# Spectral weights folded by column, projections in two pieces, and a new order at the start of an attention kernel

## The chip, the cores and the metric

The kernel runs on one NeuronCore of a Trainium2 chip. The metric is device time in microseconds (us) for one execution. The engines are TensorE (PE in the profile; PEld are its weight loads), VectorE (DVE), ScalarE (ACT), GpSimd (POOL) and SyncE (SP), which here only issues DMAs. Each engine takes its instructions in the order of the program and waits on semaphores for the others.

## The reference

A layer of two branches on the same normalized input, x of shape 2 x 2048 x 256:

```python
xn = layernorm(x)                                  # per row, eps 1e-5
q, k, v = xn @ wq, xn @ wk, xn @ wv                # 16 query heads, 4 key/value heads of 16
q, k = rope(q), rope(k)
attn = causal_softmax(q k^T / 4) v @ wo
w = w_freq_real + 1j * w_freq_imag                 # 256 x 256
ffn = real(ifft(fft(xn) @ w)) + bias
out = x + attn + ffn
```

The spectral branch is linear in xn, so it is one real 256 x 256 matrix, which the kernel builds from w and from tables of cosines (`dc`) and sines (`ds`) of the transform.

## The kernel before, in words

The rows are cut into 8 blocks of 512 (4 positions of each of 2 sequences, the sequences alternating). Block n goes through these steps. `load_x` brings x by SP's queue. `row_stats` (VectorE, lines 237 and 238) gives mean and variance, `row_power` (GpSimd, 243 and 244) the reciprocal deviation, `row_shift` (VectorE, 249) minus mean times that, and the norm (399) scales and shifts each row: on VectorE for block 0, on GpSimd for the others. `transpose_x` (411) and ScalarE's copy (414) give xnT; `features` projects it to keys and values together and to two halves of the queries, through the helper `product` (155), four matmuls of 32 columns; ScalarE copies the result to `raw` (427). `rotate` and `split` apply the rotary embedding and cut float32 into three bf16 parts (518 to 556), on VectorE for block 0, on GpSimd for the others; SP's queue stacks the parts into `qst` and `kst` (393).

Then each block has 4 units of 4 heads. For each unit `maxima` computes the scores once for the row maxima (PE 155, 627 and 631, VectorE 636), `spread` sends the maxima as three more rows of `qst` (671, 677, and 678, a DMA of ScalarE's queue), `scores` computes them again and ScalarE takes the exponential (PE 155, 734 and 738, ACT 745), and `values` multiplies by v (780). `put`, `gather`, `widen` and `scale` divide by the sums on GpSimd and its DMA queue. `output` adds the spectral product `po` with mff, the product with wo, and the residual (155 and 906).

The spectral matrix `mff` is built once, in `spectral_matrix`: four `left` groups (two sums, each for two column halves; result `ps_ff`) and two `right` groups (`ps_mff`), of 16 matmuls of 128 x 256 each. The result is needed by the first `output`. Its tables are loaded by GpSimd's queue in `load_late` (225), after block 0's power.

The rotary table is expanded by `expand` (eight broadcasts on VectorE, 293) from `trig`, loaded by SP, and turned by `turn` (PE 305, ACT 306). 48 transposes of the identity (968) run on TensorE at the start.

The order on every engine is the order in which a planner inside the kernel emits the pieces. It keeps a clock for each engine (`clock`), the time from which each result is there (`there`), adds an assumed cost for each piece (`use`, `send`), and at each step takes the piece that can start soonest, with rules for ties. Each piece carries a step from which it may run and one by which it should (`since`, `by`). So a changed cost or piece can move any later piece. Before the loop, a short part is written out by hand:

```python
    ones(0)
    for i in range(NI):
        row_stats(0, i)
    row_power(0)
    load_late()
    row_shift(0)
    order_weights()
```

TensorE's results go through three PSUM banks of the ring "st", and pairs of row maxima through two double banks of the ring "s".

## Time and profile before

| | |
|---|---|
| median of 3 runs | 925.84 us (924.08 to 927.47) |
| profiled execution, its own time | 926.44 us |
| its span in the profile | 924.7 us |
| PE busy | 904.6 us (98%) |
| DVE busy | 748.0 us (81%) |
| ACT busy | 653.7 us (71%) |
| POOL busy | 370.1 us (40%) |

The busy times are of one execution. A share over the whole span is a mean over stages with different limits; TensorE's matmuls overlap in the pipeline, so a busy TensorE need not be at its peak. The idle time of an engine counts only where others wait for it.

### The profile page before, as it was taken

How to read it: one execution, taken by the hardware profiler on the slowest of the kernel's cores; microseconds unless marked ns; L12 is line 12 of the kernel's file. 1: busy time of each engine (PE TensorE's matmuls, PEld its weight loads, DVE VectorE, ACT ScalarE, POOL GpSimd, SP SyncE). 2: the span in 40 equal slices, each digit the busy share in tenths (PEclk: the TensorE clock that was granted, in tenths of full speed). 3: DMA queues.
4: the chain of work that ended last, by engine and by line, in shares of the span. 5: the costliest groups of instructions: out<-in, count | busy, mean ns of one | idle time of the engine just before them, and what ended most of it. 6: DMA issues, size and time to landing. Idle time of an engine off the chain costs nothing.

```text
span 924.7 us, 38985 instructions
## 1 busy us (share of the span) xinstructions
PE 904.6 (98%) x17324; PEld 500.5 (54%) x17324; DVE 748.0 (81%) x1056; ACT 653.7 (71%) x1375; POOL 370.1 (40%) x556
## 2 busy tenths in 40 slices
PE   7999899999999999999999999999999999999997
PEld 4666565655555555555555555555455554645443
DVE  6878697789789996998995999979789988788601
ACT  3266565587757784888865777857688878588784
POOL 7298666824672424822236520311572021102111
PEclk9999999999999999999999999999999999999999
DMA  5435823341244011440002500010133001100000
GB/s 165 119 90 143 199 92 106 97 132 38 65 121 124 27 38 34 112 129 26 14 27 85 150 28 13 27 60 14 31 109 88 15 3 38 49 14 15 27 1 24
DMA packets 41992, 62.13 MB, mean 67 GB/s; under 512 B 8840, under 2 KB 32120, under 8 KB 41824
## 3 DMA queue, kind: packets, MB, share of 16 engines
q1 hardware_dynamic: 32400, 41.18, 16.5%
q0 software_dynamic: 8128, 17.69, 5.9%
q8 instruction: 135, 2.21, 1.0%
q10 hardware_dynamic: 1296, 0.79, 0.3%
q14 instruction: 33, 0.27, 0.1%
HBM read 32.75 MB, written 18.40 MB: 55 GB/s over the span
## 4 chain that ended last, share of the span: by engine, by line
PE 89%; DVE 5%; ACT 3%; issue 1%; DMA 1%; POOL 1%; ACTq 0%; SPq 0%; DVEq 0%; POOLq 0%
PE av L780 24%; PE st L155 22%; PE sm L155 17%; PE sm L631 7%; PE po L155 6%; PE ps_q L155 4%; DVE mx L636 2%; PE sp L155 2%; PE sm L627 2%; PE st L738 2%; ACT es L745 1%; PE ps_x L411 1%; PE st L734 1%; ACT es L747 1%; PE ps_m L671 0%
## 5 line engine op out<-in xcount | busy, mean ns | idle before, releaser
L636 DVE TENSOR_REDUCE mx<-sm 128x2 f32<-128x1024 f32 (+3 forms) x640 | 648.9, 1057 | 87.4 <-PE sm L631 44.1
L745 ACT ACTIVATE es<-st 128x512 f32<-128x512 f32 (+3 forms) x1194 | 552.4, 543 | 179.2 <-PE st L155 145.6
L155 PE MATMUL st<-qst,kst 115*32 115x512 bf16 (+3 forms) x4264 | 327.2, 354 | 1.1 <-ACT es L745 0.4
L780 PE MATMUL av<-es,va 128*32 128x512 f32 (+3 forms) x2560 | 299.9, 529 | 0.6 <-issue 0.3
L155 PE MATMUL sm<-kst,qst 112*32 112x512 bf16 x3072 | 239.1, 379 | 0.1
L155 PEld LDWEIGHTS <-kst 115*32 115x32 bf16 x4608 | 161.1, 95 | 140.6 <-issue 64.8
L752 POOL TENSOR_SCALAR_AFFINE_SELECT es<-es 128x256 f32<-128x256 f32 x192 | 76.7, 406 | 276.0 <-ACT es L745 234.8
L155 PEld LDWEIGHTS <-qst 112*32 112x32 bf16 x3072 | 96.0, 96 | 93.0 <-issue 64.8
L631 PE MATMUL sm<-kst,qst 112*32 112x32 bf16 (+15 forms) x2048 | 122.3, 281 | 0.3 <-issue 0.3
L627 PE MATMUL sm<-mask,ident_h 128*32 128x128 bf16 (+3 forms) x2048 | 100.2, 201 | 1.8 <-DVE mx L636 1.0
L780 PEld LDWEIGHTS av<-es,va 128*32 128x32 f32 x2560 | 85.1, 109 | 28.6 <-ACT avs L791 2.6
L631 PEld LDWEIGHTS <-qst 112*32 112x32 bf16 x2048 | 66.3, 97 | 34.3 <-issue 20.6
L627 PEld LDWEIGHTS <-ident_h 128*32 128x32 bf16 x2048 | 66.1, 96 | 32.2 <-issue 25.5
L906 DVE TENSOR_TENSOR xr<-po,xr 128x256 f32<-128x256 f32 x36 | 15.2, 424 | 51.5 <-PE po L155 49.5
L803 POOL DMA_DIRECT2D res<-avs x30 | 18.2, 606 | 82.7 <-ACT avs L791 79.9
L155 PE MATMUL ps_q<-xnT,wp 128*32 128x512 f32 x384 | 45.4, 600 | 0.0
L747 ACT ACTIVATE es<-sp 128x1024 f32<-128x1024 f32 (+3 forms) x43 | 36.6, 907 | 7.6 <-PE sp L155 7.4
L427 ACT COPY raw<-ps_q 128x512 f32<-128x512 f32 x24 | 14.1, 585 | 35.0 <-PE ps_q L155 35.0
L518 POOL TENSOR_TENSOR ra<-raw,cs 128x512 f32<-128x512 f32 (+1 forms) x21 | 27.4, 1304 | 24.2 <-ACT raw L427 23.0
L738 PE MATMUL st<-qst,kst 115*32 115x480 bf16 (+15 forms) x512 | 36.8, 284 | 0.1
L155 PE MATMUL po<-wo_sb,attT 128*32 128x256 f32 x512 | 34.4, 379 | 0.7 <-ACT attT L869 0.7
L155 PE MATMUL po<-mff,xnT 128*32 128x256 f32 x512 | 34.4, 380 | 0.0
(108 smaller groups left out, 657.0 us busy)
## 6 DMA issues: line engine op xcount, KB each, us to landing
qst<-run SPq DMA_DIRECT2D x62, 128.0 KB
res<-avs POOLq DMA_DIRECT2D x30, 256.0 KB, 3.0
run<-part SPq DMA_DIRECT2D x31, 192.0 KB
qst<-run SPq DMA_DIRECT2D x31, 192.0 KB
xt<-in_L_attn_x_dram SPq DMA_DIRECT2D x8, 512.0 KB
xr<-in_L_attn_x_dram SPq DMA_DIRECT2D x16, 256.0 KB
out_dram<-xr SPq DMA_DIRECT2D x16, 256.0 KB
sw<-raw SPq DMA_DIRECT2D x60, 64.0 KB
```

Of the source, the lines that this page charges most:

```text
L155: nc.tensor.matmul(to[q : q + QD], lhsT[:, q : q + QD], rhs, start=start, stop=stop)
L518: e.tensor_tensor(ra[c][:r], raw[c][:r], cs[j][:r, 0, :], ALU.mult)
L627: nc.tensor.matmul(to[:, at:wd], ident_h[:, q : q + QD], mask[:, q:], start=True, stop=True, skip_group_check=True,)
L631: nc.tensor.matmul(to[:, : at + QD], rows[:, q : q + QD], keys[:, : at + QD], start=False, stop=True, skip_group_check=True,)
L636: nc.vector.tensor_reduce(t["mx"][:, i, 2 * pr : 2 * pr + 2, k], ps[0][:, :, :wd], AX.X, ALU.max)
L738: nc.tensor.matmul(to[:, at:], keys[:, q : q + QD], rows[:, at:], start=False, stop=True, skip_group_check=True,)
L745: nc.scalar.activation(es[u, t, pr][:, e, lo:], ps[:, lo:], AF.Exp, scale=SCALE)
L747: nc.scalar.activation(es[u, t, pr][:, :, lo:], wide[pr][:, :, lo:], AF.Exp, scale=SCALE)
L752: nc.gpsimd.affine_select(out=es[u, t, pr][:, :, lo : lo + P], in_=es[u, t, pr][:, :, lo : lo + P], pattern=[[0, 2], [1, P]], compare_op=A ...
L780: nc.tensor.matmul(av[u][QD * h : QD * (h + 1), lo:], va[at_block[b, t // NI]][:, t % NI, h, :], es[u, t, h // 2][:, h % 2, lo:], start=(t ...
L803: nc.gpsimd.dma_start(out=res[n, c][f], in_=avs[u])
L906: nc.vector.tensor_tensor(xr[n, r][:, e, :], po, xr[n, r][:, e, :], ALU.add)
```

## The change

The load of block 0's x becomes four DMAs of 128 rows each, and each `row_stats` of block 0 waits for its own. The rotary table of positions 0 is expanded on VectorE right behind block 0's statistics, ahead of `row_shift`. `row_shift` becomes a plain product of mean and reciprocal deviation, which the norm subtracts, and it runs on GpSimd for blocks 1 to 7. `features` is emitted as two pieces, one for each half of the contraction, which the planner may separate. The spectral matrix uses the symmetry of cosine and sine in the column: GpSimd adds and subtracts the real and imaginary weights of column c and 256 - c (two copies and four sums, `fold`), so that two `left` groups (each of two pieces of 8 matmuls) and two `right` groups of 8 matmuls remain. A further table `half_sb`, of cosine's row 128 and sine's rows 1 to 127, is loaded by two more DMAs of GpSimd's queue, into a slot of the ring "es". The negated sine table is not made any more. The planner's costs follow.

```diff
@@ -164,10 +164,13 @@
     xt = {}
     def load_x(n):
-        send("sp", 512, [slot("xt")], [("xt", "in", n)])
+        at = slot("xt")
         take_slot("xt")
         xt[n] = work.tile([P, NI, D], F32, tag="xt", bufs=2, name=f"xt{n}")
-        nc.sync.dma_start(out=xt[n], in_=block_rows(n))
+        step = NI if n else 1
+        for i in range(0, NI, step):
+            send("sp", 128 * step, [at], [("xt", "in", n, k) for k in range(i, i + step)])
+            nc.sync.dma_start(out=xt[n][:, i : i + step, :], in_=block_rows(n)[:, i : i + step, :])
     take_slot("qst"), take_slot("qst")
     load_x(0)
@@ -224,6 +227,12 @@
             spec[name] = work.tile([P, NK, D], F32, tag=tag, bufs=bufs, name=name)
             nc.gpsimd.dma_start(out=spec[name], in_=src.rearrange("(c p) n -> p c n", p=P))
             send("pool", 256, (), ["spec"])
+        take_slot("es")
+        half_sb = spec["half"] = work.tile([P, D], F32, tag="es", bufs=ES, name="half_sb")
+        nc.gpsimd.dma_start(out=half_sb[0:1], in_=dft[0, P : P + 1, :])
+        nc.gpsimd.dma_start(out=half_sb[1:P], in_=dft[1, 1:P, :])
+        send("pool", 128, (), ["spec"])
+        send("pool", 128, (), ["spec"])
         nc.gpsimd.dma_start(out=wo_sb, in_=wo.rearrange("(c p) n -> p c n", p=P))
         nc.gpsimd.dma_start(out=bias_sb, in_=bias.partition_broadcast(P))
@@ -236,7 +245,7 @@
         st = work.tile([P, 6], F32, tag="bn", bufs=3, name=f"bn{n}_{i}")
         nc.vector.bn_stats(st, xt[n][:, i, :])
         nc.vector.bn_aggr(mv[n][:, i, :], st)
-        use("dve", 0.53, [("xt", "in", n)], [("mv", n)])
+        use("dve", 0.53, [("xt", "in", n, i)], [("mv", n)])
     def row_power(n):
         rstd[n] = work.tile([P, NI], F32, tag="rs", bufs=2, name=f"rs{n}")
@@ -246,10 +255,9 @@
     def row_shift(n):
         shift[n] = work.tile([P, NI], F32, tag="sh", bufs=2, name=f"sh{n}")
-        nc.vector.scalar_tensor_tensor(
-            shift[n], mv[n][:, :, 0], -1.0, rstd[n], ALU.mult, ALU.mult
-        )
-        use("dve", 0.2, [("rs", n)], [("sh", n)])
+        e, eng, us = (nc.vector, "dve", 0.2) if n == 0 else (nc.gpsimd, "pool", 0.25)
+        e.tensor_tensor(shift[n], mv[n][:, :, 0], rstd[n], ALU.mult)
+        use(eng, us, [("rs", n)], [("sh", n)])
@@ -310,58 +318,81 @@
         return expand, turn
     mff = const.tile([P, NK, D], F32, name="mff")
     def spectral_matrix():
-        wre, wim, dc, ds_ = (spec[k] for k in ("wre", "wim", "dc", "ds"))
-        neg_s = work.tile([P, NK, D], F32, tag="xr", bufs=3, name="neg_s")
-        at_ = work.tile([P, NK, D], F32, tag="xr", bufs=3, name="at_")
-        et_ = work.tile([P, NK, D], F32, tag="xr", bufs=3, name="et_")
-        nc.scalar.mul(neg_s, ds_, -1.0)
-        use("act", 0.48, ["spec"], ["neg_s"])
+        wre, wim, dc, ds_, half_sb = (spec[k] for k in ("wre", "wim", "dc", "ds", "half"))
         first_xr = used["xr"]
         for _ in range(3):
             take_slot("xr")
-        pieces = []
-        def left(o, name, dst, parts):
-            cols = slice(o * P, (o + 1) * P)
-            ps = bank(f"ps_ff{o}")[:, :D]
-            for a, (w, f) in enumerate(parts):
-                for c in range(NK):
-                    product(
-                        ps, w[:, c, cols], f[:, c, :],
-                        start=(a == 0 and c == 0), stop=(a == 1 and c == NK - 1),
-                    )
-            nc.scalar.mul(dst[:, o, :], ps, 1.0 / D)
-            through_bank(1.87, ["neg_s"], "act", 0.29, [("left", o, name)])
+        of_c, of_s, left_sb = (
+            work.tile([P, NK, D], F32, tag="xr", bufs=3, name=name) for name in ("vc", "vs", "left")
+        )
+        up, down, far = slice(1, P), slice(D - 1, P, -1), slice(P + 1, D)
+        pool = nc.gpsimd
+        folds = []
+        def fold(to, cols, one, two, op, last=False):
+            def go():
+                pool.tensor_tensor(to[:, :, cols], one, two, op)
+                use("pool", 0.75, ["spec"], ["folded"] * last)
+            folds.append(go)
+        def ends_of(to, w):
+            pool.tensor_copy(to[:, :, 0:D:P], w[:, :, 0:D:P])
+            use("pool", 0.2, ["spec"])
+        folds += [lambda: ends_of(of_c, wre), lambda: ends_of(of_s, wim)]
+        fold(of_c, up, wre[:, :, up], wre[:, :, down], ALU.add)
+        fold(of_s, up, wim[:, :, up], wim[:, :, down], ALU.add)
+        fold(of_c, far, wim[:, :, down], wim[:, :, up], ALU.subtract)
+        fold(of_s, far, wre[:, :, up], wre[:, :, down], ALU.subtract, True)
+        def left(o, a):
+            v, f = ((of_c, dc), (of_s, ds_))[a]
+            if a == 0:
+                held[o] = bank(f"ps_ff{o}")[:, :D], take_slot("st")
+            ps, k = held[o]
+            for c in range(NK):
+                product(
+                    ps, v[:, c, o * P : (o + 1) * P], f[:, c, :],
+                    start=(a == 0 and c == 0), stop=(a == 1 and c == NK - 1),
+                )
+            use("pe", 0.94, ["folded", ("st", k - ring["st"])], [("ps", k)])
+            if a == 1:
+                nc.scalar.mul(left_sb[:, o, :], ps, 1.0 / D)
+                use("act", 0.29, [("ps", k)], [("st", k), ("left", o)])
+        held = {}
+        lefts = [("left", o) for o in range(NK)]
         def right(r):
-            cols = slice(r * P, (r + 1) * P)
             ps = bank(f"ps_mff{r}")[:, :D]
-            for a, (w, f) in enumerate(((at_, dc), (et_, neg_s))):
-                for c in range(NK):
-                    product(
-                        ps, w[:, c, cols], f[:, c, :],
-                        start=(a == 0 and c == 0), stop=(a == 1 and c == NK - 1),
-                    )
+            for c, f in enumerate((dc[:, 0, :], half_sb)):
+                product(
+                    ps, left_sb[:, c, r * P : (r + 1) * P], f,
+                    start=(c == 0), stop=(c == NK - 1),
+                )
             nc.scalar.copy(mff[:, r, :], ps)
-            lefts = [("left", o, name) for o in range(NK) for name in ("at", "et")]
-            through_bank(1.87, lefts, "act", 0.29, [("mff", r)])
+            through_bank(0.94, lefts, "act", 0.29, [("mff", r)])
             if r == NK - 1:
                 for tag, k in (
-                    ("inv", 0), ("inv", 1), ("attT", 0), ("avs", 0),
+                    ("inv", 0), ("inv", 1), ("attT", 0), ("avs", 0), ("es", 0),
                     ("xr", first_xr), ("xr", first_xr + 1), ("xr", first_xr + 2),
                 ):
                     there[tag, k] = clock["pe"]
+        pieces = []
         for o in range(NK):
-            pieces.append((["neg_s"], lambda o=o: left(o, "at", at_, ((wre, dc), (wim, ds_)))))
-            pieces.append((["neg_s"], lambda o=o: left(o, "et", et_, ((wim, dc), (wre, neg_s)))))
-        lefts = [("left", o, name) for o in range(NK) for name in ("at", "et")]
-        for r in range(NK):
-            pieces.append((lefts, lambda r=r: right(r)))
-        return pieces
+            pieces.append((["folded"], ["st"], lambda o=o: left(o, 0)))
+            pieces.append((["folded"], [], lambda o=o: left(o, 1)))
+        pieces += [(lefts, ["st"], lambda r=r: right(r)) for r in range(NK)]
+        return folds, pieces
@@ -382,7 +413,7 @@
         b, j = blocks[n]
         e, eng = (nc.vector, "dve") if n == 0 else (nc.gpsimd, "pool")
         MULT, SUB, CAST, NORM = (0.72, 0.72, 0.46, 0.33) if n == 0 else (1.23, 1.13, 0.63, 0.53)
-        raw, sw, swp, part, ra, at = {}, {}, {}, {}, {}, {}
+        raw, sw, swp, part, ra, at, held = {}, {}, {}, {}, {}, {}, {}
         sends = []
         streams.append(sends)
@@ -398,7 +429,7 @@
         def norm(i):
             e.tensor_scalar(
                 xt[n][:, i, :], xt[n][:, i, :], rstd[n][:, i : i + 1], shift[n][:, i : i + 1],
-                ALU.mult, ALU.add,
+                ALU.mult, ALU.subtract,
             )
             use(eng, NORM, [("sh", n)], [("xn", n, i)])
@@ -416,18 +447,20 @@
             if c == NK - 1:
                 there["xt", n] = clock["pe"]
-        def features(c):
-            ps = bank(f"ps_q{n}_{c}")
-            for k in range(NK):
-                product(
-                    ps, wp[:, k, c, :], xnT[n][:, k, :], start=(k == 0), stop=(k == NK - 1)
-                )
+        def features(c, k):
+            if k == 0:
+                held[c] = bank(f"ps_q{n}_{c}"), take_slot("st")
+            ps, at_st = held[c]
+            product(ps, wp[:, k, c, :], xnT[n][:, k, :], start=(k == 0), stop=(k == NK - 1))
+            use("pe", 0.9, ["wp", ("xnT", n, k), ("st", at_st - ring["st"])], [("ps", at_st)])
+            if k < NK - 1:
+                return
             raw[c] = work.tile([P, SB], F32, tag="raw", bufs=3, name=f"raw{n}_{c}")
             at[c] = take_slot("raw")
             nc.scalar.copy(raw[c], ps)
-            through_bank(
-                1.83, ["wp", *(("xnT", n, k) for k in range(NK))], "act", 0.48, [("raw", "in", n, c)],
-                [("raw", at[c] - ring["raw"])],
+            use(
+                "act", 0.48, [("ps", at_st), ("raw", at[c] - ring["raw"])],
+                [("st", at_st), ("raw", "in", n, c)],
             )
             if n >= 2:
                 other_half(c)
@@ -568,7 +601,8 @@
         ]
         for c in (NK, 0, 1):
             table = [("cs", j, 1)] * (n >= 2)
-            pe.append(("pe", ["wp", *table, *xs], ["st", "raw"] + ["sw"] * (n >= 2), lambda c=c: features(c)))
+            pe.append(("pe", ["wp", *table, xs[0]], ["st", "raw"] + ["sw"] * (n >= 2), lambda c=c: features(c, 0)))
+            pe.append(("pe", [xs[1]], [], lambda c=c: features(c, 1)))
             if n < 2:
                 pe.append(("pe", [("raw", "in", n, c)], ["st", "sw"], lambda c=c: other_half(c)))
             if c == NK:
@@ -973,6 +1007,8 @@
         row_stats(0, i)
     row_power(0)
     load_late()
+    table_0 = rotary_table(0)
+    table_0[0]()
     row_shift(0)
     order_weights()
@@ -980,9 +1016,9 @@
         norms, pe, rot = project(n)
         eng = norms[0][0]
-        stats = [("dve", [("xt", "in", n)], [], lambda i=i: row_stats(n, i)) for i in range(NI)]
+        stats = [("dve", [("xt", "in", n, i)], [], lambda i=i: row_stats(n, i)) for i in range(NI)]
         stats.append(("pool", [("mv", n)], [], lambda: row_power(n)))
-        stats.append(("dve", [("rs", n)], [], lambda: row_shift(n)))
+        stats.append(("pool", [("rs", n)], [], lambda: row_shift(n)))
         s = starts
         if n > 1:
             stream([("sp", [], ["xt"], lambda: load_x(n))], s["load"], s["load"])
@@ -1002,10 +1038,10 @@
                 out_rot.append((at, at + late + 2 + k // 2, *p))
     def table(j, since):
-        expand, turn = rotary_table(j)
+        expand, turn = rotary_table(j) if j else table_0
         last = [("cs used", at_block[B - 1, j - 2])] if j >= 2 else []
         stream(
-            [("dve", last, ["raw", "raw2"], expand)]
+            [("dve", last, ["raw", "raw2"], expand)] * (j > 0)
             + [("pe", [("trx", j)], ["st"], lambda a=a: turn(a)) for a in range(2)],
             since, since + 3,
         )
@@ -1016,11 +1052,9 @@
     chain(1, early, 1)
     load_x_2 = stream([("sp", [], ["xt"], lambda: load_x(2))])
-    def spectral():
-        for needs, piece in spectral_matrix():
-            spectral_pieces.append((-1, 8, "pe", needs, ["st"], piece))
-    spectral_pieces = stream([("act", ["spec"], [], spectral)], -1, 8)
+    folds, products = spectral_matrix()
+    stream([("pool", ["spec"], [], fold) for fold in folds], -1, 4)
+    stream([("pe", *piece) for piece in products], -1, 8)
     for n in range(2, NB):
         at = next(k for k, d in enumerate(due) if d >= a_from[NG * n])
         starts = dict(load=at - 30, stats=at - 24, pe=at - 20, rot=at - 17)
```

## The prediction

> **What bounds the kernel now.** I read the page's busy shares first, then the busy time by stage, then the chain of waits in the stage that the diff touches, and last the timeline of that stage.
>
> ```profile
> PE 904.6 (98%) x17324; PEld 500.5 (54%) x17324; DVE 748.0 (81%) x1056; ACT 653.7 (71%) x1375; POOL 370.1 (40%) x556
> ...
> PE   7999899999999999999999999999999999999997
> ```
>
> TensorE is busy in all but 20.1 us of 924.7, so only three things can move the time: less TensorE work, fewer holes in it, or work at a better clock. Where the 20.1 us lie is seen by stage (busy us of PE, PEld, DVE, ACT, POOL; then the granted clock, the DMA share, GB/s):
>
> ```profile
> 0.00:14.00 14.00, 10.68 (x68) 9.39 (x72) 9.86 (x35) 4.96 (x11) 7.96 (x21) 0.92 0.62 184
> 14.00:23.70 9.70, 8.28 (x68) 2.03 (x67) 6.45 (x13) 2.58 (x5) 8.45 (x16) 0.94 0.42 134
> 23.70:46.00 22.30, 21.74 (x472) 14.05 (x464) 18.38 (x42) 6.26 (x13) 6.87 (x11) 1.00 0.43 120
> ...
> 100.00:140.00 40.00, 36.18 (x1028) 25.97 (x1029) 32.80 (x62) 24.00 (x65) 25.47 (x39) 0.96 0.47 131
> ...
> 900.00:924.70 24.70, 18.52 (x268) 8.91 (x260) 3.23 (x8) 13.08 (x17) 3.23 (x8) 0.97 0.07 23
> ```
>
> Holes: 3.3, 1.4 and 0.6 us up to 46 us, 3.8 us between 100 and 140, 6.2 us in the tail, little elsewhere. In the first row 7.1 us of the busy time is the 48 warm-up transposes, which end at 8.55. So up to 46 us about 5.3 us stand open and the rest is real work. The chain of waits there:
>
> ```profile
> 0.80 4.43 DMA xt<-in_L_attn_x_dram
> ...
> 7.90 1.06 POOL rs L244
> 8.96 0.02 issue
> 8.98 0.16 DVE sh L249
> 9.14 1.17 DVE trx L293 x6
> 10.31 0.04 issue
> 10.36 1.11 PE ps_tr L305 x8
> 11.47 0.10 issue
> 11.56 2.32 PE ps_x L411 x8
> 13.88 2.54 PE ps_q L155 x16
> ```
>
> The reader is to see that VectorE waits for GpSimd's power (1.5 us), and only then builds the rotary table (1.63 us for eight), which does not need the power at all. The norms start at 10.61, behind the table. The second thing is the clock (same columns as above):
>
> ```profile
> 8.40:10.40 2.00, 0.20 (x3) 0.04 (x1) 1.42 (x8) 1.13 (x4) 2.00 (x3) 1.00 0.00 0
> ...
> 11.40:15.00 3.60, 3.49 (x17) 1.83 (x20) 3.10 (x12) 1.90 (x4) 3.54 (x7) 0.55 0.86 281
> ```
>
> After the empty 1.81 us from 8.55 to 10.36 the clock is 0.55 for 3.6 us. The third is block 1, seen on GpSimd's and VectorE's timeline:
>
> ```profile
> 33.42 0.23 POOL L243 TENSOR_SCALAR rs<-mv 128x4 f32<-128x4 f32 x1 [10.62 <-DVE mv L238]
> ...
> 33.81 0.15 DVE L249 SCALAR_TENSOR_TENSOR sh<-mv,rs 128x4 f32<-128x4 f32 x1
> ...
> 34.78 4.30 POOL L399 TENSOR_SCALAR xt<-xt,rs,sh 128x256 f32<-128x256 f32 x8
> ```
>
> Block 1's power was done at 20.1, but its shift sits in VectorE's queue behind block 0's rotation (17.06 to 31.04) and runs at 33.81. GpSimd is empty for 10.6 us, then has block 1's norms, and from 44.5 on its rotation.
>
> **The change, part by part.** The profiled execution took 926.44 us (span 924.7 and 1.7 around it). The median of the three runs is 925.84, 0.6 less and within their spread; I sum against the execution and take the difference off the median.
>
> *Half the products.* Before, 4 left groups and 2 right groups of 16 matmuls of 128x256 each, 96 in all; after, 4 pieces and 2 groups of 8, 48 in all. Rate from the timeline, where a full group starts 0.86 us before the next one:
>
> ```profile
> 23.70 1.05 PE L155 MATMUL ps_ff<-dc,wre 128*32 128x256 f32 x16
> ...
> 24.56 1.05 PE L155 MATMUL ps_ff<-ds,wim 128*32 128x256 f32 x16
> ```
>
> 0.86 / 16 = 54 ns; 48 x 54 ns = 2.6 us less for TensorE. ScalarE loses the negation (0.63) and two evictions (0.38 each), worth nothing on a 71% engine.
>
> *What the fold adds.* On GpSimd two small copies and four sums of 2x127 columns. No such row exists (reversed source). Nearest are a 128x512 sum at 1.28 and a 256-wide scale at 0.55. Bounds 0.55 and 1.3 each; I take 0.7, so 4 x 0.7 + 0.4 = 3.2 us (2.6 to 5.6). Below nothing is excluded, since it is only added. Two more loads by GpSimd's queue, 0.72 each like their neighbours, stand ahead of wo, the bias and block 1's memsets: 1.4 us. Cover: GpSimd's 10.6 empty us. Without it block 1's norms come 4.6 us later, and TensorE with them.
>
> *First load in four.* VectorE's memsets end at 4.63, the statistics now start at 5.25 on the whole load and step at 0.53. With pieces the first can start at 4.65, and the fourth ends at 6.8 instead of 7.48 if the last piece lands by 6.2: 0.7 less. SP issues three more DMAs of 0.44, so the rotary table's load and block 1's x leave 1.3 us later. They are first needed at 6.8 and 10.5. The DMA engines are full from 3 to 7 us (share 1.07 to 1.11) and empty from 8, so all first loads still land by about 8 in whatever order. Here the Trainium skill speaks against the change: "DMA: Bandwidth & Descriptors", section Bandwidth, wants transfers batched to 1 MiB, and its section on the anatomy of one DMA gives 2.0 us fixed for each. Taken one after another, four would need 0.8 + 4 x (2.0 + 0.3) and land at 10, costing the front some 3.5 us, and the sum below would be -0.9. The row shows several loads of different queues in flight at full share, so the fixed parts should overlap. I take the row; 0 to 0.7 us gained.
>
> *Table ahead of the shift.* VectorE: statistics to 6.8, table 1.63 to 8.45, while GpSimd takes its 1.4 us to 8.3; shift 0.16, norms 1.89 to 10.5, where they now end at 12.5. That is 2.0 us. What is late next is the fourth norm, then two evictions of ScalarE (0.59 each). If the table's load came after 8.3, shift and norms would queue behind it, us for us.
>
> *The clock.* The table's transposes follow the warm-up at 8.6 with no gap to speak of. The skill's "TensorE: Matmul & The Clock Gate", section on HAM oscillation, warns only of idle gaps above about 3.4 us; by it a gap of 1.81 is harmless and closing it gains nothing. The trace differs: 0.55 right after 1.81. From the fourth norm to the first projection's end take 3.9 us now (12.5 to 16.42); at full clock two evictions, 0.3 for the transposes, 0.86 for the second half and 0.3 of latency need 2.9. So 1.0 by the row, nothing by the rule. Together the front chain is 3.0 us earlier (2.0 by the rule).
>
> *Shift on GpSimd for blocks 1 to 7.* Seven times 0.25 on an engine at 40%, 0.15 less on VectorE. Its effect is the order: power, shift and norms of block 1 follow each other, after two blocks' memsets (2.5 each) and the two loads: norms end near 22 instead of 37. The new multiply has no negation; the norm subtracts instead, same cost. The later blocks save little, except one 1.0 us wait of the shift at 228, where VectorE is on the chain.
>
> *Projections in two pieces.* The same matmuls. A PSUM bank of the three can be held between the pieces while others are scheduled, and the later pieces may be planned up to two steps later. Bounds: -1 (better mixing) to +2; no row shows it, I take 0, since two banks already let a 0.54 us eviction alternate with 0.2 us of scores.
>
> *New holes in the front.* Block 0's rotation on VectorE still takes 14 us from the first raw copy, so row maxima start near 28.5 instead of 31.46. Until then TensorE has block 0's projections, then block 1's transposes at 22, then spectral pieces when the fold ends, about 26. Between 20.8 and 23.5 there is less to do than now, when the spectral lefts (23.3 to 31.4) fill: I charge 1.2 us (0 to 4).
>
> Sum: -3.0 - 2.6 + 1.2 = -4.4 us; 922.0 for the execution, 921.4 for the median.
>
> **The rivals.** *More than that:* block 1's GpSimd work begins up to 18 us earlier, which loosens what follows. The one big later hole is
>
> ```profile
> 106.87 0.24 PE L734 MATMUL st<-mask_t,ident_h 128*32 128x128 bf16 x4 [2.19 <-issue]
> ```
>
> where a unit's maxima had been sent only at 103.19 and the clock falls to 0.66 (106 to 111). If the new order avoids it, 2.2 and some 1.4 of slow clock go: -8.0, 917.8. Against it: any new order can have such a hole of its own.
>
> *Filler only:* TensorE waits for block 0's rotation anyway, so the products saved become holes: the sum is -3.0 + 1.2 = -1.8, 924.0. For it: VectorE is busy without a break from 17 to 31. Against: block 1 now supplies some 9 us of work there.
>
> *The fold starves TensorE:* TensorE's order is fixed, and the spectral pieces stand in it where the kernel's planner expects the fold (0.75 per sum; loads of wo and bias not counted). If the fold ends 6 us after TensorE reaches them (sums at 1.3 us, another block's memsets ahead), everything behind waits: 6.0 and 1.7 of halved clock against the 4.4 gained, -4.4 + 7.7 = +3.3, 929.1. It decides from about 4 us of lag. For it: GpSimd carries 4.6 us more just there. Against: 10.6 us empty.
>
> **How the numbers follow.** The measurement tells 0.3% (2.8 us) from no change. Chances: the sum 0.50, more than it 0.20, filler 0.15, starvation 0.15. The sum's own unknowns (fold, pieces, holes, load) make it 918.5 to 925, a sixth of it inside 0.3%. Faster 0.42 + 0.20 + 0.02, same 0.08 + 0.12, slower 0.01 + 0.15. The range reaches from beyond the second case (916.5) over the third to half way into the fourth (927.5).
>
> **What would show it.** Right: the table's transposes at 8.6 and a clock near 1.0 from 11 to 15; first projection done near 13.4; block 1's norms on GpSimd before 24 and a fold of some 3.2 us behind them; 48 spectral matmuls; TensorE busy about 902, span about 920. Wrong: a spectral matmul waiting on GpSimd for more than 3 us, statistics waiting past 7 for the last piece, a halved clock after 20 us, new waits for PSUM banks, or holes of over 2 us after 46 us.

## The result, and the profile after

The changed kernel is slower: 937.79 us (932.05 to 940.0, 6 runs) against 926.83 us (924.08 to 927.66, 6 runs), a ratio of 1.0113 with an interval of 1.0082 to 1.0143. The prediction had 921.4.

The page of the changed kernel, busy time and share of each engine:

```profile
PE 903.8 (97%) x17228; PEld 495.0 (53%) x17228; DVE 748.2 (80%) x1049; ACT 653.9 (70%) x1372; POOL 397.0 (42%) x571
```

TensorE is busy 0.8 us less than before, but over a span of 935.0 us: its holes have grown from 20.1 to 31.2 us. GpSimd is busy 26.9 us more, where the prediction added some 6. By stage (busy us of PE, PEld, DVE, ACT, POOL; then granted clock, DMA share, GB/s):

```profile
0.00:14.00 14.00, 11.84 (x80) 9.65 (x80) 10.04 (x37) 5.82 (x12) 8.59 (x22) 1.00 0.61 184
14.00:23.70 9.70, 7.16 (x60) 1.73 (x60) 8.60 (x14) 1.70 (x4) 9.28 (x17) 1.00 0.57 172
23.70:46.00 22.30, 16.94 (x303) 8.80 (x307) 14.97 (x33) 4.21 (x9) 19.31 (x24) 0.85 0.31 86
...
100.00:140.00 40.00, 33.78 (x995) 22.69 (x987) 32.42 (x60) 25.04 (x67) 28.24 (x40) 0.96 0.53 136
140.00:200.00 60.00, 58.15 (x1102) 32.90 (x1093) 43.65 (x64) 30.85 (x65) 40.57 (x49) 0.97 0.34 96
```

The first row is better than before, as forecast: 1.2 us fewer holes and a whole clock. The second has 1.1 us more holes. The third has 5.4 us of holes instead of 0.6, and the clock is 0.85. Then come 2.4 us more holes from 100 to 140, and 1.9 from 140 to 200, where there were none. The chain of waits of the first 50 us (start, us, what) shows who holds TensorE up:

```profile
9.98 0.94 PE ps_x L442 x4
10.94 0.59 ACT xnT L445
11.57 1.97 PE ps_q L155 x16
13.56 0.59 ACT raw L460
...
24.26 0.57 POOL sh L259
24.83 0.14 POOL vc L347
24.98 5.32 POOL xt L430 x4
30.34 1.33 PE ps_x L442 x5
31.66 2.69 PE ps_q L155 x16
```

Four norms on GpSimd take 5.32 us on the chain. And TensorE's own rows there (start, us, operation, idle before it and for what):

```profile
26.26 0.33 PE L442 MATMUL ps_x<-ident,xt 128*128 128x128 f32 x1 [3.49 <-POOL xt L430]
27.70 0.47 PE L442 MATMUL ps_x<-ident,xt 128*128 128x128 f32 x1 [1.11 <-POOL xt L430]
29.13 0.48 PE L442 MATMUL ps_x<-ident,xt 128*128 128x128 f32 x1 [0.95 <-POOL xt L430]
30.34 1.33 PE L442 MATMUL ps_x<-ident,xt 128*128 128x128 f32 x5 [0.73 <-POOL xt L430]
```

TensorE stands 6.3 us before block 1's transposes, and block 0's row maxima stand behind them in its queue. The clock pays again right after:

```profile
26.00:30.00 4.00, 1.28 (x3) 0.50 (x3) 3.79 (x10) 0.00 (x0) 4.00 (x4) 0.56 0.39 99
30.00:34.00 4.00, 3.67 (x21) 1.59 (x25) 0.52 (x3) 1.17 (x2) 3.06 (x6) 0.58 0.77 208
```

The reason shows in the row of the norm itself, by its tile (min, median and max ns):

```profile
L430 POOL TENSOR_SCALAR xt<-xt,rs,sh x28: 1212/1215/1449, 25.0 to 660.1; 128x256 f32<-128x256 f32 x28
```

The same row before is this, for the same shape and count:

```profile
L399 POOL TENSOR_SCALAR xt<-xt,rs,sh x28: 545/548/561, 34.8 to 650.7; 128x256 f32<-128x256 f32 x28
```

A norm that multiplies and subtracts takes GpSimd 1.215 us, one that multiplies and adds 0.548 (medians). 28 x 0.667 = 18.7 us, most of what GpSimd has gained. TensorE's waits on it are 10.5 us in all, close to the growth of its holes.

### The profile page after: what moved, and what is told of

It reads as the page before. It is cut to its first block, busy times and chain, and to the rows that moved or that the text cites. A ratio compares the mean times of both kernels' runs of the same rounds, so it can differ in the third digit from the quotient of the medians.

```text
span 935.0 us, 38841 instructions
## 1 busy us (share of the span) xinstructions
PE 903.8 (97%) x17228; PEld 495.0 (53%) x17228; DVE 748.2 (80%) x1049; ACT 653.9 (70%) x1372; POOL 397.0 (42%) x571
## 4 chain that ended last, share of the span: by engine, by line
PE 85%; POOL 5%; ACT 3%; DVE 3%; DMA 2%; issue 2%; SPq 0%; ACTq 0%; POOLq 0%; DVEq 0%
PE av L814 23%; PE st L155 22%; PE sm L155 17%; PE sm L665 6%; PE po L155 5%; PE ps_q L155 4%; POOL xt L430 3%; ACT es L779 2%; PE sp L155 2%; PE sm L661 1%; DVE mx L670 1%; PE st L772 1%; PE ps_x L442 1%; PE idle L1002 1%; ACT es L781 1%
## 5 line engine op out<-in xcount | busy, mean ns | idle before, releaser
L155 PE MATMUL st<-qst,kst 115*32 115x512 bf16 (+3 forms) x4264 | 331.4, 354 | 0.8
L155 PEld LDWEIGHTS <-kst 115*32 115x32 bf16 x4608 | 158.7, 95 | 153.6 <-issue 79.2
L665 PE MATMUL sm<-kst,qst 112*32 112x64 bf16 (+15 forms) x2048 | 120.8, 280 | 2.3 <-issue 2.3
L814 PEld LDWEIGHTS av<-es,va 128*32 128x32 f32 x2560 | 85.3, 110 | 30.3 <-issue 3.8
L661 PE MATMUL sm<-mask,ident_h 128*32 128x64 bf16 (+3 forms) x2048 | 99.1, 201 | 0.8 <-DVE mx L670 0.4
L155 PE MATMUL ps_q<-xnT,wp 128*32 128x512 f32 x384 | 49.6, 609 | 0.3 <-ACT xnT L445 0.2
L155 PE MATMUL po<-wo_sb,attT 128*32 128x256 f32 x512 | 36.2, 394 | 0.7 <-ACT attT L903 0.7
L551 POOL TENSOR_TENSOR ra<-raw,cs 128x512 f32<-128x512 f32 (+1 forms) x21 | 26.9, 1280 | 20.5 <-ACT raw L460 19.7
L772 PE MATMUL st<-qst,kst 115*32 115x512 bf16 (+15 forms) x512 | 35.6, 284 | 0.0
L430 POOL TENSOR_SCALAR xt<-xt,rs,sh 128x256 f32<-128x256 f32 x28 | 34.4, 1235 | 0.6 <-POOL sh L259 0.2
```

The costliest lines, as they stand in the source:

```text
L155: nc.tensor.matmul(to[q : q + QD], lhsT[:, q : q + QD], rhs, start=start, stop=stop)
L430: e.tensor_scalar(xt[n][:, i, :], xt[n][:, i, :], rstd[n][:, i : i + 1], shift[n][:, i : i + 1], ALU.mult, ALU.subtract,)
L551: e.tensor_tensor(ra[c][:r], raw[c][:r], cs[j][:r, 0, :], ALU.mult)
L661: nc.tensor.matmul(to[:, at:wd], ident_h[:, q : q + QD], mask[:, q:], start=True, stop=True, skip_group_check=True,)
L665: nc.tensor.matmul(to[:, : at + QD], rows[:, q : q + QD], keys[:, : at + QD], start=False, stop=True, skip_group_check=True,)
L772: nc.tensor.matmul(to[:, at:], keys[:, q : q + QD], rows[:, at:], start=False, stop=True, skip_group_check=True,)
```

## The experiments

Theory A: the form of the norm is the loss. Theory B: the new order is. Each run below is compared with the kernel before on the same chip; a ratio below 1 is faster than the kernel before. The runs were taken on several chips, so two runs are set against each other by their ratios; 0.1% is 0.9 us.

**e1: the changed kernel, but the norm adds.** GpSimd negates the shift with one more small operation. The order on TensorE is that of the changed kernel.

```diff
-        e.tensor_tensor(shift[n], mv[n][:, :, 0], rstd[n], ALU.mult)
+        if n == 0:
+            e.scalar_tensor_tensor(
+                shift[n], mv[n][:, :, 0], -1.0, rstd[n], ALU.mult, ALU.mult
+            )
+        else:
+            e.tensor_tensor(shift[n], mv[n][:, :, 0], rstd[n], ALU.mult)
+            e.tensor_scalar(shift[n], shift[n], -1.0, None, ALU.mult)
...
-                ALU.mult, ALU.subtract,
+                ALU.mult, ALU.add,
```

> The changed kernel in its own order, but the norm multiplies and adds again; GpSimd negates the shift with one more small operation per block (about 0.25 us). Theory A (the slow form of the norm): the norm falls from 1.22 us to the 0.55 it had, TensorE's waits on it fall from 10.5 us to under 2, the halved clock between 26 and 34 us goes, and the time is 920 to 925. Theory B (the new order as such loses): the norm's duration falls too, but the time stays above 931, since holes between 70 and 200 us remain.

Measured: 929.63 us, ratio 1.0036 (1.0021 to 1.0051). The norm is back at a median of 550 ns, and some 7 us of the loss are gone (ratio 1.0113 to 1.0036). But the time lies between what A and B expected. TensorE's two longest waits are now these (in all, times, longest):

```profile
PE st L774 <- ACT es L785: 5.7, 4, 4.4
PE ps_x L448 <- POOL xt L436: 4.9, 4, 3.9
```

The second, 4.9 us, stands before block 1's norm. GpSimd's timeline of e1 shows why the norm is late even when it is fast:

```profile
20.19 1.04 POOL L253 TENSOR_TENSOR rs<-rs,neg_half 128x4 f32<-128x4 f32 x1
21.20 0.52 POOL L410 MEMSET va<- 128x512 f32 x1
21.78 2.36 POOL L413 MEMSET kst<- 32x512 bf16 x4
24.21 0.57 POOL L264 TENSOR_TENSOR sh<-mv,rs 128x4 f32<-128x4 f32 x1
24.88 0.25 POOL L265 TENSOR_SCALAR sh<-sh 128x4 f32<-128x4 f32 x1
25.08 0.18 POOL L353 COPY vc<-wre 128x4 f32<-128x4 f32 x1
25.26 3.42 POOL L436 TENSOR_SCALAR xt<-xt,rs,sh 128x256 f32<-128x256 f32 x4
```

Block 1's four norms take 3.42 us, where four at the median would take 2.2; VectorE is busy for 3.33 of the 3.50 us from 25.2 on. Between block 1's power and its shift stand the memsets of a third block, and a copy of the fold behind the shift. The code says how they get in: the planner gives a result free 0.12 us after its operation (`LATE`), and picks by due step only among pieces that can start within 0.1 us of the soonest. A shift that depends on the operation just emitted is thus passed over for anything that is ready.

The first wait has its long part, 4.4 us, at 115.7, and it comes from ScalarE's queue (timeline; the last row is from the chain of waits):

```profile
113.21 0.57 ACT L717 COPY mt<-ps_m 12x512 bf16<-12x512 bf16 x1 [0.16 <-PE st L778]
118.93 0.73 ACTq L718 DMA_DIRECT2D qst<-mt  x1
119.70 1.27 ACT L785 ACTIVATE es<-st 128x256 f32<-128x256 f32 x5 [5.91 <-DMA xr<-in_L_attn_x_dram]
...
112.36 6.49 DMA xr<-in_L_attn_x_dram
```

A unit's maxima are ready at 113.8, but their DMA leaves only at 118.9. By the semaphores of the trace ScalarE stood there until a load of x for a residual had landed, which SP had issued and which took 6.49 us; the exponentials behind it stood too, and TensorE behind them. The clock is 0.50 from 117.1 to 123.9. The changed kernel has the same wait, with 3.4 us of ScalarE idle.

**e2: the kernel before, in its own order, but the norm subtracts.**

```diff
-            shift[n], mv[n][:, :, 0], -1.0, rstd[n], ALU.mult, ALU.mult
+            shift[n], mv[n][:, :, 0], 1.0, rstd[n], ALU.mult, ALU.mult
...
-                ALU.mult, ALU.add,
+                ALU.mult, ALU.subtract,
```

> The kernel before in its own order, with only the sign of the shift turned and the norm subtracting it. Theory A: GpSimd's norm goes from 0.55 to about 1.2 us, 28 times, and TensorE waits where transposes stand close behind it, above all for block 1; 928 to 933. Theory B: GpSimd has room, the order is the old one, 926 to 928.

Measured: 940.46 us, ratio 1.0154 (1.013 to 1.0178), more than A expected. One operator, and the loss is larger than that of the whole change. TensorE's waits on the norm are many and short here:

```profile
PE ps_x L411 <- POOL xt L399: 7.8, 11, 0.9
```

The copies of the value sums (one per unit, counted from 0) show a staircase against the kernel before: the first is 5.6 us late, the one of unit 8 7.1, of 16 10.1, of 20 11.7, and from unit 25 on it stays at 13.4. Each later step, where another block's norms fall, costs 1.1 to 1.9 us, and from unit 8 on nothing gives it back. So the form of the norm alone suffices; theory B is not needed for a loss of this size.

**e3: the slow norm kept, the planner told.** Only a number of the planner changes; the instructions are those of the changed kernel in another order.

```diff
-        MULT, SUB, CAST, NORM = (0.72, 0.72, 0.46, 0.33) if n == 0 else (1.23, 1.13, 0.63, 0.53)
+        MULT, SUB, CAST, NORM = (0.72, 0.72, 0.46, 0.33) if n == 0 else (1.23, 1.13, 0.63, 1.3)
```

> The changed kernel with the slow norm kept, but the kernel's planner is given 1.3 instead of 0.53 us for it, so that TensorE's order is planned for it. Theory A, with the loss in TensorE standing in its queue behind transposes that came too early: waits on the norm fall from 10.5 to under 4 us, and the time comes to 926 to 931. If it is GpSimd's work itself that is too much, or the new order, it stays at 935 or above.

Measured: 926.68 us, ratio 1.0000 (0.9985 to 1.0016). The norms still take 1.216 us and GpSimd is busy 396.5 us, but all of the loss, some 10 us, is gone. What costs is not GpSimd's work but where TensorE's queue stands still for it. The waits fell less than expected, to 6.6 us, all four in the front.

**e4: the forms by themselves.** The kernel before, and behind GpSimd's last operation a row of `tensor_scalar` with two operators, twice each, then three with one:

```diff
+    for one, two in (
+        (ALU.mult, ALU.add), (ALU.mult, ALU.subtract), (ALU.subtract, ALU.mult),
+        (ALU.add, ALU.mult), (ALU.mult, ALU.mult), (ALU.add, ALU.add),
+    ):
+        for _ in range(2):
+            nc.gpsimd.tensor_scalar(junk, junk, side[:, 0:1], side[:, 1:2], one, two)
```

> The kernel before, and behind its last GpSimd operation a row of two-operation norms of 128x256 on a spare tile: multiply-add, multiply-subtract, subtract-multiply, add-multiply, multiply-multiply, add-add, and single operations. Theory A1: every pair with a subtraction takes about 1.2 us and the others 0.55. A2: only multiply-add has a fast form, and all other pairs take about 1.2. B: all take about 0.55, and the 1.2 of the changed kernel came from contention with other engines. The time itself stays within 1 us of before, since GpSimd is empty at the end.

GpSimd's timeline, one row of each of the six pairs in that order, and the first of the single multiplications:

```profile
914.28 0.56 POOL L1212 TENSOR_SCALAR junk<-junk,neg_half 128x256 f32<-128x256 f32 x1
...
914.94 1.24 POOL L1212 TENSOR_SCALAR junk<-junk,neg_half 128x256 f32<-128x256 f32 x1
...
917.59 1.23 POOL L1212 TENSOR_SCALAR junk<-junk,neg_half 128x256 f32<-128x256 f32 x1
...
920.24 0.55 POOL L1212 TENSOR_SCALAR junk<-junk,neg_half 128x256 f32<-128x256 f32 x1
...
921.54 0.56 POOL L1212 TENSOR_SCALAR junk<-junk,neg_half 128x256 f32<-128x256 f32 x1
...
922.85 1.25 POOL L1212 TENSOR_SCALAR junk<-junk,neg_half 128x256 f32<-128x256 f32 x1
...
925.52 0.93 POOL L1215 TENSOR_SCALAR junk<-junk,neg_half 128x256 f32<-128x256 f32 x1
```

Multiply-add, add-multiply and multiply-multiply take 0.55 us; multiply-subtract, subtract-multiply and add-add take 1.23; a single operator, whether multiply, add or subtract, takes 0.93, more than a fast pair. Neither A1 nor A2 holds: fast is a pair that has a multiplication and no subtraction, and the pair of two additions is slow without any. It is no contention: from 922.8 to 925.4, where add-add runs at 1.25, no other engine is busy. The one time of 942.0 says nothing, since the row runs on past the kernel's own end.

**e5: e1 with the memsets of blocks 2 and 3 later.**

```diff
-        starts["ones"] = 0 if n < 4 else 8 * n - 26
+        starts["ones"] = 4 if n < 4 else 8 * n - 26
```

> The changed kernel with the adding norm (as in e1), and the memsets of blocks 2 and 3 planned from step 4 instead of step 0, so that on GpSimd block 1's power, shift and norms follow each other. Theory C (TensorE's queue stands still at block 1's transposes, with block 0's row maxima behind them, because GpSimd fills 2.9 us of memsets and a fold copy in between): the hole of 3.9 us before 26.4 and the halved clock after it go, and the time falls from 929.6 by 4 to 6, to 924 to 926. Theory D (the remaining loss of e1 lies in holes after 70 us that any new order brings): no gain beyond 2 us.

Measured: 929.33 us, ratio 1.0025 (1.001 to 1.0041). The hole did go: from 23.7 to 46 us TensorE is busy 22.0 of 22.3 us, where e1 has 18.7. Block 1's norms end at 23.1. The median did not follow. But the profiled execution, at 924.44, is the fastest of 19 and within what theory C expected, so its profile can't say what the usual ones lose, nor whether the hole is closed in them. C's time is not borne out by the median; that the hole costs nothing is not shown.

**e6, e7, e8, e9: one part each, on the kernel before.** e6 has the hunks of `load_late`, `spectral_matrix` and its streams; e7 those of `load_x`, `row_stats` and the table ahead of the first shift; e8 those of `features`; e9 has those of `row_shift` in e1's form. In short:

```diff
# e6
+        nc.gpsimd.dma_start(out=half_sb[1:P], in_=dft[1, 1:P, :])
+    folds, products = spectral_matrix()
# e7
+        step = NI if n else 1
+    table_0 = rotary_table(0)
+    table_0[0]()
     row_shift(0)
# e8
-        def features(c):
+        def features(c, k):
# e9
-        stats.append(("dve", [("rs", n)], [], lambda: row_shift(n)))
+        stats.append(("pool", [("rs", n)], [], lambda: row_shift(n)))
```

> The kernel before with only the folded spectral weights, half the products, and the two loads they need. By the prediction's terms: 2.6 us less for TensorE, the fold in GpSimd's empty time: 924. If the products were only filler while TensorE waits for block 0's rotation: 926 to 927. If the fold or the later spectral pieces hold TensorE up: above 928.

> The kernel before with only the load of block 0's x in four, and the rotary table ahead of the first shift. By the prediction's terms the front is 3.0 us earlier and the clock stays whole: 923 to 924. If TensorE's work of the front is only moved into a later hole: 926 to 927.

> The kernel before with only the projections in two pieces each. By the prediction's terms no change, 925 to 928. If a bank of three held between the pieces starves the scores, ScalarE's exponentials and TensorE wait for each other: 929 to 932.

> The kernel before with only the shift of blocks 1 to 7 on GpSimd (in the fast form: product, negated by one more small operation, norm adds). By the prediction's terms block 1's norms end some 10 us earlier at no cost: 925 to 926. If taking block 1 forward puts its transposes into TensorE's queue ahead of block 0's row maxima while GpSimd still fills memsets (as in e1): 928 to 931.

| part alone | median us | ratio | interval |
|---|---|---|---|
| e6 fold | 938.64 | 1.0134 | 1.0113 to 1.0156 |
| e7 front | 924.28 | 0.9971 | 0.9957 to 0.9986 |
| e8 pieces | 926.15 | 1.0002 | 0.9989 to 1.0015 |
| e9 shift, fast form | 926.35 | 0.9996 | 0.998 to 1.0012 |

e7 has a gain close to the forecast 3.0: 0.29% or 2.7 us, with an interval of 1.3 to 4.0. TensorE's program in it is, instruction for instruction, that of the kernel before, so no change of order is mixed in. The clock in its first rows:

```profile
0.00:14.00 14.00, 12.21 (x80) 10.23 (x80) 10.61 (x37) 5.45 (x12) 8.55 (x22) 1.00 0.64 190
14.00:23.70 9.70, 8.42 (x92) 3.00 (x96) 8.23 (x14) 2.97 (x6) 7.83 (x15) 1.00 0.44 146
```

The whole clock is not e7's doing. e2 has the front of the kernel before, with the table behind the shift, and in its profile the clock is whole as well (TensorE's first row behind the warm-up, and the stretch that the prediction read at 0.55):

```profile
10.41 1.09 PE L305 MATMUL ps_tr<-ident,trx 128*128 128x128 f32 x8 [1.23 <-DVE trx L293]
...
11.40:15.00 3.60, 3.14 (x25) 1.37 (x24) 3.19 (x12) 1.86 (x4) 3.54 (x8) 1.00 0.83 262
```

The same 48 warm-up transposes took 7.77 us there and 7.14 in the profile before, so the hole behind them was 1.23 us and not 1.80. e6, e9 and e16 have this front too, holes of 1.06 to 1.25, and a clock of 1.00 in this stretch.

e6 was the surprise: no slow norm in it, and 12 us lost. GpSimd's timeline of e6 (in the program, the first norm is block 2's, the second block 1's):

```profile
35.65 2.17 POOL L428 TENSOR_SCALAR xt<-xt,rs,sh 128x256 f32<-128x256 f32 x4 [0.97 <-DVE sh L255]
49.12 2.16 POOL L428 TENSOR_SCALAR xt<-xt,rs,sh 128x256 f32<-128x256 f32 x4 [11.31 <-DVE sh L255]
```

With the fold in, the planner emits block 2's shift and norm ahead of block 1's, whose shift on VectorE came only at 48.87, behind the row maxima. So block 1's norm ends at 51.3 instead of 39. What TensorE then waits for, between 100 and 140 us, are rows of `qst` that arrive late:

```profile
PE st L767 <- DMA qst<-mt: 6.0, 2, 3.1
```

TensorE is busy 17.4 of 22.3 us from 23.7 to 46, and 31.5 of 40 from 100 to 140. For the fold itself it waits once, 1.7 us. So the trace puts e6's loss on the order; no run with the fold in the old order tests it.

**e10, e11, e12: the company of the parts.** e10 is e1 without the fold's hunks, e11 is e10 with e5's line, e12 is e5 without the hunks of `features`.

> e1 without the fold: front, pieces and shift on GpSimd, the spectral matrix as before with twice the products. If the fold costs more than its products save even in this company, it is faster than e1's 929.6, at 925 to 928. If the fold saves what the prediction said, it is slower by 1 to 3 us, 931 to 933.

> e10 with the memsets of blocks 2 and 3 from step 4. The version that the parts point to: the front's 2.5 us kept, no fold in GpSimd's queue, block 1's norms early. 921 to 924 if the holes behind block 1's norm are what remained; 926 or more if the new order makes holes of its own after 70 us whatever GpSimd does.

> e5 without the projections in two pieces: front, fold, shift in the fast form, memsets later. If the pieces are neutral as in e8, it stays within 2 us of e5's 929.3. If pieces held in a PSUM bank are what keeps e5 above the kernel before, 924 to 926.

Measured: e10 930.14 us (1.0033, 1.0021 to 1.0044), e11 930.32 (1.0032, 1.0017 to 1.0046), e12 933.59 (1.0071, 1.0048 to 1.0094). Without the fold the rest is as far above the kernel before as with it (e1 has 1.0036): in this company no cost or gain of the fold is seen, though the orders differ too. e11 was meant as the version that beats both, and missed. e12 contradicts the guess that pieces hurt: without them it is slower, again in another order. The parts do not add up: e6, e7, e8 and e9 sum to +1.03%, while e1, which has all four, is at +0.36%.

**e13, e17, e16: the same instructions in another order.** Only the norm's cost in the planner's table changes: in e1 to 1.3 (e13; TensorE's stream is e3's) and 0.8 (e17), in the kernel before to 0.60 (e16).

> e1 (all parts, adding norm) with the planner given 1.3 us for GpSimd's norm although it takes 0.55: TensorE's order is exactly that of e3. Theory E (the rest of the loss is TensorE's order, planned for a GpSimd that keeps up): e3's 926.7 less what its slow norms still cost there, so 920 to 924, below the kernel before. Theory F (the parts together cost something real, such as the fold and the extra loads): no better than e3, 926 to 929.

> The same with 0.8 us planned for the norm. Theory E: between e1's 929.6 and e13. If it lies outside both, by more than 2 us, the order's effect is not a matter of room but of chance.

> The kernel before with the same instructions, only the planned cost of GpSimd's norm 0.60 instead of 0.53, which reorders a tenth of TensorE's stream. If an order alone moves the time by about what separates e1 from the kernel before: 924 to 932, outside 926 to 928. If orders are equivalent: 926 to 928.

Measured: e13 926.17 us (0.9991, 0.9977 to 1.0005), e17 925.28 (0.9979, 0.9967 to 0.999), e16 927.81 (0.9999, 0.9982 to 1.0016). From e1 to e17 nothing changes but the order, and some 5 us go (0.57%). The two profiles, first e1's rows and then e17's, show where:

```profile
14.00:46.00 32.00, 25.72 (x414) 11.88 (x412) 25.00 (x48) 6.69 (x13) 28.55 (x45) 0.89 0.41 119
100.00:140.00 40.00, 32.40 (x956) 21.70 (x950) 29.88 (x55) 23.24 (x63) 27.17 (x40) 0.91 0.49 129
```

```profile
14.00:46.00 32.00, 25.71 (x424) 12.00 (x422) 25.99 (x49) 6.47 (x13) 29.23 (x45) 0.89 0.49 139
100.00:140.00 40.00, 36.72 (x1054) 24.93 (x1048) 35.22 (x60) 23.07 (x62) 28.23 (x42) 1.00 0.49 140
```

The front is the same; from 100 to 140 us e17 has 3.3 us of holes instead of 7.6, and the clock is whole instead of 0.91. ScalarE's long stand at its own DMA, shown for e1, is not there: each of e17's sends of maxima in this stretch leaves right behind its copy. e13, with e3's order and fast norms, is no faster than e3 within their intervals, so by its own expectation theory E is not borne out there. e17 is beyond both e1 and e13, by about 1 us from e13. e16 shows that an order alone need not matter.

**e18, e19: the two remedies together.** e18 is e17 with e5's later memsets. e19 is e5 with a planner that counts what it had left out:

```diff
         nc.gpsimd.dma_start(out=bias_sb, in_=bias.partition_broadcast(P))
+        use("pool", 1.4)
...
-        e, eng, us = (nc.vector, "dve", 0.2) if n == 0 else (nc.gpsimd, "pool", 0.25)
+        e, eng, us = (nc.vector, "dve", 0.2) if n == 0 else (nc.gpsimd, "pool", 0.65)
...
-        MULT, SUB, CAST, NORM = (0.72, 0.72, 0.46, 0.33) if n == 0 else (1.23, 1.13, 0.63, 0.53)
+        MULT, SUB, CAST, NORM = (0.72, 0.72, 0.46, 0.33) if n == 0 else (1.23, 1.13, 0.63, 0.6)
```

> e17 (all parts, adding norm, 0.8 us planned for it) with the memsets of blocks 2 and 3 from step 4, as in e5. If the front's hole and its halved clock are what is left: 925.3 less 4 to 5, so 920 to 922, the predicted time. If the hole only moves behind block 1, as from e1 to e5: 924 to 927.

> e5 with a planner that counts the two loads behind the tables (1.4 us), the negation with its shift (0.65), and 0.6 for the norm, so that plan and GpSimd agree. If room as such was the remedy in e17, this is as good or better: 920 to 924. If e17's order was good by chance: 926 to 930, like e5.

Measured: e18 927.48 us (1.0015, 1.0002 to 1.0028), e19 925.63 (0.9995, 0.9984 to 1.0007). e18 missed. The hole before block 1's norm is gone, but in its profile (its time was 930.11, above the median) it has moved behind block 1, where TensorE waits for VectorE's row maxima and the clock is halved at 36.2:

```profile
35.56 0.22 PE L667 MATMUL sm<-mask,ident_h 128*32 128x128 bf16 x4 [3.39 <-DVE mx L676]
```

e19 has that hole too (3.54 us at 32.0). It is better than e5 by 0.3%, but not better than the kernel before. Two versions beat both kernels: e7, with the front alone (0.9971), and e17 (0.9979). No version reached the predicted 921.4.

## Why the prediction was wrong, point by point

*The norm, the step that failed.* "The new multiply has no negation; the norm subtracts instead, same cost." It was costed at nothing without a row for that form; 0.55 was carried over from a row of another pair of operators. The form costs 1.215. e2 puts 13.8 us on it in the old order, e1 some 7 in the new one; in the order that e3 and e13 share, planned for a slow norm, the two forms differ by 0.1%, within the intervals. So the loss is the slow form in an order that does not expect it. It is about half of the miss: of the 1.6% between the forecast (0.9952) and the result (1.0113), 0.8% goes with the form, and 0.8% stays in e1. The fourth rival had the right place, TensorE's fixed queue standing behind GpSimd with the clock halved after it, but named the fold for it, with a lag from the sums. The fold took what was forecast: 0.72, 0.73, 0.64, 0.72 and two copies of 0.18 and 0.19, 3.2 us.

*Half the products, mis-sized.* The step took 54 ns for a matmul. But each of these float32 matmuls is two records in the trace: the rows of x16 were 8 matmuls, half a group, as their names say (`dc,wre` and `ds,wim` are the two halves of one sum). The page has 96 records fewer (17324 to 17228), so the saving is 96 x 54 ns = 5.2 us and not 2.6. In some runs it shows: TensorE is busy 899.3 us in e1 and 898.1 in e3 against 904.6; where more of the work runs at a halved clock, as in the changed kernel (903.8), it does not. Yet no run turned it into time: e10, with all the products, is as fast as e1, and in e6 the time goes up. On an engine that is 98% busy, less work was still worth nothing in these orders, each of which has new holes.

*The front, right but for its clock term.* Statistics done at 6.9 (forecast 6.8), norms at 10.5 (10.5), first raw copy at 13.56 (13.4), the clock 1.00 up to 23.7. One detail was off: the table waited 0.49 us for its load, which the split had put 1.4 us later. Of the two rules that the prediction weighed against rows, the one on DMAs lost: no statistics waited for a piece. (The 2.0 us of the Trainium skill's "DMA: Bandwidth & Descriptors", in the section on the anatomy of one DMA, are for DMAs issued from GpSimd; these were SP's.) On the clock gate nothing is decided. The term of 1.0, the row taken against the rule, rested on one execution. With the same front e2, e6, e9 and e16 had a whole clock and the first raw copy at 15.2 to 15.7, not 16.45, so the change brings it forward by about 2 us there. e7's gain of 2.7 (1.3 to 4.0) can't tell 2.0 from 3.0; that it came near 3.0 may be luck. The parts that the prediction lists for the stretch from the fourth norm to the first projection's end also add up to 2.6, not 2.9; it took 3.05 (10.51 to 13.56).

*Shift on GpSimd, half right.* It did bring block 1 forward, but its norms end at 30.3, not 22. In e1, with the fast form, they end at 28.7. The memsets were counted for two blocks ahead of it; a third block's came between power and shift. With those moved away, in e5, the norms do end near the forecast, at 23.1. (Before, they ended at 39.1, not 37: block 2's four stand between them.) By itself (e9) it is neutral, as forecast.

*Pieces, right by themselves* (e8): no change.

*Holes in the front, mis-sized.* 1.2 us (0 to 4) were charged; TensorE waited 6.3 for the norm, and 4.9 in e1, with two halved windows behind.

*What stays open.* e1 is at +0.36% with no slow form in it. e17 shows that another order takes this back, and the traces name the largest single difference between the two: ScalarE's stand of 5 us at a DMA of its own, with the halved clock behind it. Whether removing that wait alone would do it was not run. e5, e12, e18 and e19 have other holes in other places, so which property of an order makes the holes between 70 and 140 us is not settled in general.

## What to carry to other kernels

Before an operator is exchanged for its mirror image (add for subtract, a sign moved to the other operand), find a row of exactly that form on that engine, or measure it: on GpSimd a factor of 2.2 hung on it. In a kernel whose order comes from a planner, a changed part moves all the rest, so the parts' own times do not add; hold the order still (e1, e2) to measure an operation, and hold the operations still (e13, e16, e17) to measure the order. When a rate is read from a trace, count records against the instructions of the program first. And before a gain is put on a stretch of low clock, see whether a second profile with the same front has it.

## What the runs showed of the hardware that was not expected

- GpSimd's `tensor_scalar` on 128x256 float32 with two operands per partition: 0.55 us for multiply-add, add-multiply and multiply-multiply, 1.23 for multiply-subtract, subtract-multiply and add-add, 0.93 with one operator. The same multiply-add took up to 1.06 in e1 in a stretch where VectorE was busy. VectorE shows no such step: its four norms with the subtraction take 0.41 (0.44 with the addition).
- TensorE's clock was halved after holes of 1.8 us (before, at 10.4), 2.2 (before, at 106.9) and 3.5 (after, at 26.3; 0.56 and 0.58 over the next 8 us). It stayed at 1.00 after holes of 1.9 (e11, at 99.3) and 3.1 (e6, at 123.8), and in e5 it was 0.53 from 23.4 to 27 behind waits of at most 0.7. So these runs give no length of a hole that decides, and a halved stretch in one profile need not be there in the next.
- A DMA that ScalarE issues can hold up its exponentials: in e1 it left 5.1 us after its data were ready, behind a load on SP's queue.
- Runs of the same program differ by up to 0.9% here, and the mean granted clock goes with it: the kernel before ran from 923.3 at 1.000 to 931.6 at 0.993 in one session.
